# First attention: order of logits, values and other pieces on TensorE, and the banks they use

## The chip, the core and the metric

One core of a Trainium2 chip runs the whole program. Its engines are TensorE (PE: matrix products), VectorE (DVE), ScalarE (ACT), GpSimd (POOL) and SyncE (SP, which here only issues transfers). Each engine works through its own list of instructions in order and waits on semaphores for the others. TensorE writes its products into PSUM, which has eight banks of 128 partitions x 512 float32; the other operands lie in SBUF. The metric is the time of one execution in microseconds on the device. An execution is timed several times, and the median counts; one execution is also profiled.

## What is computed

Two transformer layers on x of 4 batches x 1024 rows x 256 columns, each with an attention and a mixture of experts, both behind a layer norm that is scaled and shifted per batch (adaLN). The change touches the first attention, in which 16 heads of 16 columns share one latent key and value of 64 columns:

```python
Q = (hidden_states @ Wq.T).reshape(b, t, h, d)
latent_k = hidden_states @ Wk_down.T
latent_v = hidden_states @ Wv_down.T
q_lat = jnp.einsum('bthd,hdl->bthl', Q, q_to_latent)
logits = jnp.einsum('bthl,bsl->bhts', q_lat, latent_k) / math.sqrt(l)
logits = jnp.where(causal[None, None], logits, jnp.float32(-1e+30))
attn = jax.nn.softmax(logits, axis=-1)
ctx_lat = jnp.einsum('bhts,bsl->bhtl', attn, latent_v)
heads = jnp.einsum('bhtl,hld->bthd', ctx_lat, v_up)
out = heads.reshape(b, t, h * d) @ Wout.T
```

The expert layer behind it takes the two best of 16 experts for each row: a router's logits, a softmax, a sort of the rows by expert, then two products per row with a layer norm and a gelu between. Its routing and sorting for the batches that are ready are done while the attention still works on the later batches.

## The kernel before

**Units.** The kernel multiplies the key and value weights into 256-column ones once, so that a head has 16 key columns and 16 value columns of its own. It goes through 4 batches x 2 halves of the heads (`g`) x 2 sets (`o`: the even or the odd ones of the eight heads of a half) x 9 units: 144 units, in the list `units` (L436). A unit (`UNITS`, L232) is a block of 512 columns of queries against one block of 128 keys, or two smaller blocks that together have 512 columns, for four heads at once. `scores` (L380) makes the logits of a unit with 4 or 8 products that each use 32 rows of the array, into two tiles `ps_s` of two banks each (L383); ACT takes the exponential of each of the two tiles into a tile `pT` (L396, 7 buffers), and POOL sets the upper triangle to 0 in the diagonal units (L399).

**Sums.** `sums` (L441) is a generator over the value products in order. One chunk, 512 queries of four heads, is accumulated in one bank `ps_av` (L448): 4 or 8 pieces of a unit, listed in `SUMS` (L244), each of four products that use 32 columns of the array (L453). Before each piece it yields the number of the unit whose exponentials the piece needs. When the chunk is complete, `finish` (L407) transposes it on DVE (L411), takes the reciprocal of the sums of the exponentials (L413) and scales (L414); every second time it transposes back (L416). At the end of a batch the generator appends the projection (`project`, L420) and, through `after_batch`, the routing of the batch (`Experts0.rows`, L1101) and after every second batch the sort (`Experts0.sort`, L1117) to the list `around`.

**Other work.** `around` is a list of generators, and a step (`Around.step`, L44) runs the first of them to its next `yield`. Between two yields lies a piece. Large pieces are the products for the values (`ps_v`, L349), for queries and keys (`ps_qk`, L364) and of the projection (`ps_out`, L427), each filling one bank. Small ones are the transpositions of normalised rows (`ps_lnT`, L153 and L1057), the router's products (`ps_route`, L794, and `ps_logits`, L802) and the sort's (`ps_rank`, `ps_expert`, `ps_gain`). Others only give work to DVE (statistics, normalising). `prepare` (L341) for the next half of the heads is put at the head of the list. Besides, `riders` scatter the sorted rows to memory, one transfer from POOL's queue for each step (L1158, L964); each is tied to the logits before it by `paced` (L980).

**Banks.** `ps_s` has three tiles of two banks, `ps_o` one bank for the sums, `ps_m` one for the other work. A `Spread` object (L275) hands out the tile for a piece: during the first and the last part (`early`) three of four come from `ps_s`, in the loop all from `ps_m`.

**Order.** An ordering pass, the planner, puts the instructions of each engine in an order of its own, by priority (their place in the text) and its own estimate of when each is ready. Inside `manual_schedule` the named engines keep the order of the text; before the change this is POOL alone. The loop (L472) does per turn: the value pieces of all units up to n - 2, the logits of unit n, one piece of other work (two in every fourth turn of the middle batches), one rider. After the loop come the last values, the projection of the last batch, and the experts (`Experts0.run`, L1178), whose weights are loaded by SP into memory that the attention leaves.

Of the kernel before, what the change touches and what calls it, by code (L numbers as in the profile page):

```python
# [8 lines left out]
F32 = mybir.dt.float32  # L9
# [4 lines left out]
PSUM = bass.MemoryType.PSUM  # L14

P = 128
B, N, C = 4, 1024, 256
NT = N // P
CC = C // P
# [14 lines left out]
class Around:  # L34
# [9 lines left out]
    def step(self, pieces=1, rides=1):  # L44
        pieces -= self.over
        while pieces > 0 and self.tasks:
            done = next(self.tasks[0], None)
            if done is None:
                self.tasks.pop(0)
            else:  # L50
                pieces -= done
        self.over = max(-pieces, 0)
        for _ in range(rides):
            if self.riders and next(self.riders[0], self) is self:
                self.riders.pop(0)

    def finish_tasks(self):
        while self.tasks:
# [192 lines left out]
def attention0(ctx, k, a, after_batch=lambda b: None):  # L251
# [18 lines left out]
    k.work = work = ctx.enter_context(k.tc.tile_pool(name="a0_work", bufs=2, reuse_waits="tile"))  # L270
    ps_s = ctx.enter_context(k.tc.tile_pool(name="a0_ps_s", bufs=3, space=PSUM, reuse_waits="tile"))
    ps_o = ctx.enter_context(k.tc.tile_pool(name="a0_ps_o", bufs=1, space=PSUM, reuse_waits="tile"))
    ps_m = ctx.enter_context(k.tc.tile_pool(name="a0_ps_m", bufs=1, space=PSUM, reuse_waits="tile"))

    class Spread:  # L275


        early, turn = True, 0

        def tile(self, shape, dtype, tag=None, name=None):  # L280
            self.turn += 1
            if self.early and self.turn % 4:
                full = ps_s.tile([P, 2, 512], dtype, tag="s", name=name)[:, 0, :]
            else:
                full = ps_m.tile([P, 512], dtype, tag="m", name=name)
            size = 1
            for n in shape[1:]:
                size *= n
            full = full[: shape[0], :size]
            if len(shape) == 2:  # L290
                return full
            names = "abc"[: len(shape) - 1]
            return full.rearrange(
                f"p ({' '.join(names)}) -> p {' '.join(names)}", **dict(zip(names, shape[1:]))
            )
# [1 line left out]
    misc = Spread()  # L297


    raw = work.tile([L, 4, C], F32, tag="pT", name="raw", bufs=7)  # L300
    wkd, wvd, q2l, vup = (raw[:, i, :] for i in range(4))
    for dst, name in ((wkd, "wkd"), (q2l, "q2l"), (wvd, "wvd"), (vup, "vup"), (wq, "wq"), (wo, "wo")):
        nc.scalar.dma_start(dst, a[name])
    k.load_c()

    def load_mod(layer):
        rest = work.tile([P, 2, 512], F32, tag="pT", name="mod_rows", bufs=7)
        w = []
        for i in range(3):
            w.append(work.tile([P, CC, 512], F32, tag="pT", name="wmod", bufs=7))  # L310
            nc.sync.dma_start(w[i], a[f"wmod{layer}"][:, :, i * 512 : (i + 1) * 512])
        return w, rest[:, 0], rest[:, 1, :C], rest[:, 1, C:]

# [66 lines left out]
    def scores(b, g, o, u):  # L380
# [11 lines left out]
                ).ins  # L392
        pTs = []
        for ps in pair:
            pT = work.tile([P, 2, 512], F32, tag="pT", name="pT", bufs=7)
            nc.scalar.activation(pT, ps, AF.Exp, scale=1.0 / L**0.5)  # L396
            for _, _, c0, _, diagonal in UNITS[u]:
                if diagonal:
                    nc.gpsimd.affine_select(  # L399
                        out=pT[:, :, c0 : c0 + P], in_=pT[:, :, c0 : c0 + P],  # L400
                        compare_op=ALU.is_ge, fill=0.0, base=0,
                        pattern=[[0, 2], [1, P]], channel_multiplier=-1,
                    )
            pTs.append(pT)
        return pTs

    def finish(b, g, o, qc, po, onT):  # L407


        turned = work.tile([P, 16, 32], F32, tag="turned", name="turned")  # L410
        nc.vector.transpose(turned.rearrange("p n d -> p (n d)"), po)  # L411
        rec = recs[:, 8 * b + 4 * g + 2 * o + qc].rearrange("p i j -> p (i j)")
        nc.vector.reciprocal(rec, turned[:, :, D])  # L413
        nc.vector.tensor_tensor(mixed[qc][:, :, o], turned[:, :, :D], bcast(rec, 2, D), ALU.mult)  # L414
# [26 lines left out]
    def sums():  # L441

        for b in range(B):
            on = ons[b % 2]
            for g in range(2):
                for o in range(2):
                    for qc, pieces in enumerate(SUMS):
                        po = ps_o.tile([P, 512], F32, tag="o", name="ps_av")  # L448
                        for n, (u, i) in enumerate(pieces):
                            yield place[b, g, o, u]  # L450
                            kb, _, c0, w, _ = UNITS[u][i]
# [14 lines left out]
    k.around.finish_tasks()  # L466
    setup_mod(k, 1, misc, mod)
    misc.early = False
    with k.tc.manual_schedule(engines={mybir.EngineType.Pool}):
        summing = sums()  # L470
        wanted = next(summing)
        for n, (b, g, o, u) in enumerate(units):  # L472
            if n == 8:
                k.clear_rows()
            if (o, u) == (0, 0):
# [2 lines left out]
                coming = (b, 1) if g == 0 else (b + 1, 0)  # L478
                if coming[0] < B:
                    around.insert(0, prepare(*coming))  # L480
            while wanted is not None and wanted <= n - 2:
                wanted = next(summing, None)
            exps[b, g, o, u] = scores(b, g, o, u)
            k.around.step(2 if b in (1, 2) and n % 4 == 3 else 1)
        misc.early = True
        for _ in summing:
            pass
        while projects[-1] in around:
# [587 lines left out]
class Experts0:  # L1076
# [24 lines left out]
    def rows(self, b, scalar):  # L1101

        k, rt = self.k, self.rt
        hf, i = divmod(b, HB)
        if i == 0:
            self.scale, self.shift = (
                spread_rows(k, rt, 0, part, 1, name, HB * hf, HB)
                for part, name in ((SCALE, "scale_f0"), (SHIFT, "shift_f0"))
            )
            self.logits = rt.tile([P, HT, E0], F32, tag="logits", name="logits")  # L1110
        statistics = yield from row_statistics(k, self.work, b)
        yield from routed_rows(
            k, self.work, b, statistics, self.scale[:, i], self.shift[:, i],
            self.wr, self.br, E0, self.logits[:, i * NT : (i + 1) * NT], scalar,
        )

# [1070 lines left out]
```

## Time and profile before

| What | us |
|---|---|
| runs | 1089.41, 1083.16, 1086.05 |
| median of the runs | 1086.05 |
| profiled execution | 1087.63 |
| its span | 1085.8 |
| first logits of the loop start | 45.1 |
| last values of the attention start | 507.0 |
| TensorE busy from 40 to 510 us | 454.0 of 470 |
| ACT, DVE and POOL busy from 40 to 510 us | 295.7, 180.2, 145.1 |
| granted TensorE clock from 40 to 510 us | 0.99 of full speed |

The span is the time from the first to the last recorded instruction; the execution's time has 1.8 us more around it. Times in the traces are microseconds from the span's start. A matrix product in float32 leaves two records, so a piece of four products has eight (x8). The ends of products are modelled by the profiler, since they run in a pipeline; what can be trusted is the distance from one start to the next. A releaser behind an arrow (<-) is the instruction whose end ended a wait.

### The profile page before, as it was taken

The numbers are of one execution on the slowest core, as the hardware profiler recorded it, in microseconds if no ns is written. First come the engines' busy times: TensorE is split into PE (matmuls) and PEld (weight loads), VectorE is DVE, ScalarE is ACT, GpSimd is POOL, SyncE is SP. The second block draws the span as 40 slices with busy tenths as digits, with TensorE's granted clock in tenths as the row PEclk, the third lists the DMA queues.
The fourth block names the chain that finished last, engine by engine and source line by source line (L and its number), as shares of the span: only waits on it lengthen the run. The fifth ranks groups of instructions, "written<-read, shape, count | busy, mean of one in ns | idle before, by whom it ended". The sixth has DMA issues, their size and how long they took to land.

```text
span 1085.8 us, 18090 instructions
## 1 busy us (share of the span) xinstructions
PE 945.7 (87%) x6072; PEld 559.8 (52%) x6072; DVE 620.4 (57%) x1987; ACT 602.5 (55%) x959; POOL 336.0 (31%) x528
## 2 busy tenths in 40 slices
PE   4899999999999999889679989986997989858760
PEld 2434434443443434335568878874464656547550
DVE  5822235422465155413676767993899968564572
ACT  0368655765477555775555657766654745523430
POOL 2013211311232234663004615612550100553632
PEclk9999999999999999999899999998999899989875
DMA  6995000100010001552825556624223201458764
GB/s 206 358 346 179 1 1 6 40 1 1 1 64 1 1 30 54 201 215 78 317 88 170 197 177 189 196 75 144 67 65 148 88 2 39 141 170 264 240 205 130
DMA packets 97142, 132.89 MB, mean 122 GB/s; under 512 B 8536, under 2 KB 84216, under 8 KB 96528
## 3 DMA queue, kind: packets, MB, share of 16 engines
q1 hardware_dynamic: 84656, 97.27, 26.9%
q0 software_dynamic: 11776, 33.57, 9.9%
q8 instruction: 52, 0.85, 0.3%
q10 hardware_dynamic: 608, 0.79, 0.3%
q14 instruction: 50, 0.41, 0.1%
HBM read 67.85 MB, written 63.75 MB: 121 GB/s over the span
## 4 chain that ended last, share of the span: by engine, by line
PE 63%; DVE 19%; issue 5%; DMA 5%; ACT 4%; POOL 1%; SPq 1%; DVEq 0%; ACTq 0%; POOLq 0%
PE ps_s L388 13%; PE ps_av L453 12%; PE ps_qk L364 6%; PE ps_y L1312 5%; PE ps_h L1247 4%; PE ps_v L349 3%; PE ps_out L427 3%; PE ps_pr L1609 3%; PE ps_y L1938 3%; PE ps_q L1537 2%; PE ps_k L1511 2%; DVE y L1601 2%; DMA ys<-results,index 2%; PE ps_lnT L1057 1%; DVE st L1258 1%
## 5 line engine op out<-in xcount | busy, mean ns | idle before, releaser
L396 ACT ACTIVATE pT<-ps_s 128x1024 f32<-128x1024 f32 x288 | 279.3, 1022 | 169.7 <-PE ps_s L388 167.2
L399 POOL TENSOR_SCALAR_AFFINE_SELECT pT<-pT 128x256 f32<-128x256 f32 x256 | 104.2, 431 | 328.4 <-ACT pT L396 323.7
L388 PE MATMUL ps_s<-qT,kT 32*128 32x512 f32 (+3 forms) x1536 | 178.8, 523 | 0.1
L453 PE MATMUL ps_av<-pT,v 128*32 128x512 f32 (+3 forms) x1536 | 165.2, 497 | 9.4 <-DVE turned L411 5.6
L964 POOL DMA_INDIRECT sorted<-hs,index x96 | 96.2, 1002 | 144.9 <-PE ps_y L1312 73.0
L974 POOL DMA_INDIRECT ys<-results,index x96 | 102.7, 1070 | 119.0 <-DMA results<-y 43.6
L388 PEld LDWEIGHTS ps_s<-qT,kT 32*128 32x128 f32 x1536 | 74.5, 185 | 95.5 <-issue 72.8
L453 PEld LDWEIGHTS ps_av<-pT,v 128*32 128x32 f32 x1536 | 40.6, 108 | 104.0 <-issue 58.7
L1247 PE MATMUL ps_h<-w,xT 128*128 x352 | 82.1, 386 | 6.5 <-DVE mv L1259 3.8
L1312 PE MATMUL ps_y<-w,act 128*128 x352 | 83.7, 392 | 4.2 <-DVE rs_seed L84 2.8
L411 DVE STREAM_TRANSPOSE turned<-ps_av 128x512 f32<-128x512 f32 x32 | 22.8, 712 | 98.9 <-PE ps_av L453 98.6
L1312 PEld LDWEIGHTS ps_y<-w,act 128*128 128x128 f32 x352 | 67.7, 197 | 14.0 <-ACT act L1295 4.8
L1247 PEld LDWEIGHTS ps_h<-w,xT 128*128 128x128 f32 x352 | 66.2, 193 | 15.9 <-issue 4.2
L1295 ACT ACTIVATE act<-ps_hT,gain 128x128 f32<-128x128 f32 x176 | 63.6, 463 | 16.9 <-PE ps_hT L1286 16.8
L1270 ACT ACTIVATE hid<-hid,nmr,rstd 128x256 f32<-128x256 f32 x88 | 47.5, 603 | 39.4 <-DVE nmr L1263 39.2
L1511 PE MATMUL ps_k<-wqkv,hT 128*128 128x512 f32 x128 | 61.9, 603 | 3.6 <-DMA wqkv<-in_wqkv_dram 2.8
L1938 PE MATMUL ps_y<-we,xT 128*128 x200 | 53.0, 412 | 10.6 <-ACT xT L1930 8.4
L371 DVE COPY qT<-ps_qk 128x512 f32<-128x512 f32 x16 | 11.0, 688 | 81.8 <-PE ps_qk L364 81.8
L103 DVE BATCH_NORM_STATS2 ln_st<-x 128x6 f32<-128x256 f32 x128 | 49.2, 407 | 0.5
L1255 DVE TENSOR_TENSOR hid<-ps_h,b 128x256 f32<-128x256 f32 x88 | 33.9, 415 | 26.6 <-PE ps_h L1247 21.5
L1938 PEld LDWEIGHTS ps_y<-we,xT 128*128 128x128 f32 x200 | 38.2, 204 | 20.1 <-ACT xT L1930 11.6
L374 DVE TENSOR_SCALAR kT<-ps_qk,par 128x512 f32<-128x512 f32 x32 | 22.5, 745 | 37.0 <-PE ps_qk L364 37.0
(223 smaller groups left out, 1499.4 us busy)
## 6 DMA issues: line engine op xcount, KB each, us to landing
xs<-sorted SPq DMA_DIRECT2D x69, 256.0 KB, 3.8
results<-y SPq DMA_DIRECT2D x69, 256.0 KB, 3.0
sorted<-zero SPq DMA_DIRECT2D x2, 6016.0 KB, 20.1
rows_in<-h SPq DMA_DIRECT2D x16, 512.0 KB, 2.9
hs<-rows_in POOLq DMA_DIRECT2D x32, 256.0 KB, 3.5
w<-in_w_dram SPq DMA_DIRECT2D x8, 1024.0 KB, 11.3
x<-in_x_dram SPq DMA_DIRECT2D x4, 1024.0 KB, 6.5
b<-in_b_dram SPq DMA_DIRECT2D x2, 2048.0 KB
```

What stands on the lines that cost most here:

```text
L364: nc.tensor.matmul(ps, lhsT=w[:, cc, g * P : (g + 1) * P], rhs=hT[:, cc, hf * 512 : (hf + 1) * 512], start=cc == 0, stop=cc == CC - 1,)
L388: k.anchor = nc.tensor.matmul(pair[hh // 2][:, hh % 2, c0 : c0 + w], lhsT=kTs[o][rows, kb * P : (kb + 1) * P], rhs=qT[rows, q1 - w : q1], ...
L396: nc.scalar.activation(pT, ps, AF.Exp, scale=1.0 / L**0.5)
L399: nc.gpsimd.affine_select(out=pT[:, :, c0 : c0 + P], in_=pT[:, :, c0 : c0 + P], compare_op=ALU.is_ge, fill=0.0, base=0, pattern=[[0, 2], [ ...
L453: nc.tensor.matmul(po[32 * hh : 32 * hh + 32, 512 - w :], lhsT=vs[b % 2][:, kb, 8 * g + 2 * hh + o, :], rhs=exps[b, g, o, u][hh // 2][:, h ...
L964: i = self.k.nc.gpsimd.indirect_dma_start(out=buffer.ap, out_offset=bass.IndirectOffsetOnAxis(ap=index, axis=0), in_=rows, in_offset=None, ...
L974: self.paced(self.k.nc.gpsimd.indirect_dma_start(out=rows, out_offset=None, in_=buffer.ap, in_offset=bass.IndirectOffsetOnAxis(ap=index, a ...
L1247: mm = nc.tensor.matmul(ph[:, j], lhsT=xTs[i // 2][:, j, cc], rhs=w1[:, cc, bass.ds(at[i + j], C)], start=cc == 0, stop=cc == CC - 1,)
L1295: o = nc.scalar.activation(act[:, j, cc], pt[:, j, cc], AF.Gelu, bias=gain[:, 1, cc, t : t + 1], scale=gain[:, 0, cc, t : t + 1],)
L1312: mm = nc.tensor.matmul(po[:, j], lhsT=acts[i // 2][:, j, cc], rhs=w2[:, cc, bass.ds(at[i + j], C)], start=cc == 0, stop=cc == CC - 1,)
L1511: k.anchor = nc.tensor.matmul(ps, lhsT=hT[:, cc, t * P : (t + 1) * P], rhs=wqkv[:, cc, C:], start=cc == 0, stop=cc == CC - 1,).ins
L1938: k.anchor = nc.tensor.matmul(po[:, j], lhsT=xT[:, j, cc], rhs=self.we[:, cc, bass.ds(at[j], C)], start=cc == 0, stop=cc == CC - 1,).ins
```

## The change

1. Sums and other work share two banks, `bank0` and `bank1`. Every chunk of the sums reverses the list: the sums take `banks[0]`, the other work `banks[1]`. In the loop the first piece of a turn uses `banks[1]`, the second a tile of `ps_s`.
2. The loop makes the logits of unit n first. Then, unless the last turn asks for a rest, and as long as the next value piece needs a unit later than n - 3, it runs other work until two pieces with a tile have been done, or one with a router's or sort's product that others wait for (`last`), or pieces without a tile worth more than 1. With a single task left it does one large piece only. Only in a turn without a tile do the values follow: of all units up to n - 1, or of unit n - 2 alone where that is the next. After a turn with small pieces the next one rests, which lets the values come.
3. TensorE too keeps the order of the text.
4. `pT` gets 8 buffers. The room for it comes from `turned` (one buffer instead of two) and from the rows of scale and shift for the expert layer's norm, which are loaded for each batch by itself instead of for two batches together.
5. The transposition of a finished chunk on DVE is given high priority.

```diff
+    def piece(self):
+        while self.tasks:
+            done = next(self.tasks[0], None)
+            if done is not None:
+                return done
+            self.tasks.pop(0)
+        return 0
...
-    ps_m = ctx.enter_context(k.tc.tile_pool(name="a0_ps_m", bufs=1, space=PSUM, reuse_waits="tile"))
+    banks = [ps_o.tile([P, 512], F32, tag=f"bank{i}", name=f"bank{i}") for i in range(2)]
     class Spread:
-        early, turn = True, 0
+        early, turn, large, last = True, 0, 0, False
         def tile(self, shape, dtype, tag=None, name=None):
             self.turn += 1
-            if self.early and self.turn % 4:
+            self.large += name in ("ps_v", "ps_qk", "ps_out")
+            self.last = name in ("ps_route", "ps_rank", "ps_expert")
+            if self.turn % 4 if self.early else self.turn % 2 == 0:
                 full = ps_s.tile([P, 2, 512], dtype, tag="s", name=name)[:, 0, :]
             else:
-                full = ps_m.tile([P, 512], dtype, tag="m", name=name)
+                full = banks[1]
...
-            pT = work.tile([P, 2, 512], F32, tag="pT", name="pT", bufs=7)
+            pT = work.tile([P, 2, 512], F32, tag="pT", name="pT", bufs=8)
...
-        turned = work.tile([P, 16, 32], F32, tag="turned", name="turned")
-        nc.vector.transpose(turned.rearrange("p n d -> p (n d)"), po)
+        turned = work.tile([P, 16, 32], F32, tag="turned", name="turned", bufs=1)
+        with k.tc.high_priority():
+            nc.vector.transpose(turned.rearrange("p n d -> p (n d)"), po)
...
-                        po = ps_o.tile([P, 512], F32, tag="o", name="ps_av")
+                        banks.reverse()
+                        po = banks[0]
...
-    with k.tc.manual_schedule(engines={mybir.EngineType.Pool}):
+    with k.tc.manual_schedule(engines={mybir.EngineType.Pool, mybir.EngineType.PE}):
         summing = sums()
-        wanted = next(summing)
+        wanted, rest = next(summing), False
         for n, (b, g, o, u) in enumerate(units):
...
-            while wanted is not None and wanted <= n - 2:
-                wanted = next(summing, None)
             exps[b, g, o, u] = scores(b, g, o, u)
-            k.around.step(2 if b in (1, 2) and n % 4 == 3 else 1)
+            misc.turn = misc.large = quiet = 0
+            misc.last = False
+            while not rest and wanted > n - 3 and misc.turn < 2 and not misc.last:
+                if misc.large and len(around) < 2:
+                    break
+                done = misc.turn
+                quiet += k.around.piece()
+                if misc.turn == done and (done or quiet > 1 or not around):
+                    break
+            k.around.step(0)
+            if not misc.turn:
+                end = n if wanted != n - 2 else n - 1
+                while wanted is not None and wanted < end:
+                    wanted = next(summing, None)
+            rest = misc.turn > misc.large and wanted < n
         misc.early = True
+        k.around.step(1, 0)
...
+        scale, shift = (
+            spread_rows(k, rt, 0, part, 1, name, b, 1)[:, 0]
+            for part, name in ((SCALE, "scale_f0"), (SHIFT, "shift_f0"))
+        )
         if i == 0:
-            self.scale, self.shift = (
-                spread_rows(k, rt, 0, part, 1, name, HB * hf, HB)
-                for part, name in ((SCALE, "scale_f0"), (SHIFT, "shift_f0"))
-            )
             self.logits = rt.tile([P, HT, E0], F32, tag="logits", name="logits")
         statistics = yield from row_statistics(k, self.work, b)
         yield from routed_rows(
-            k, self.work, b, statistics, self.scale[:, i], self.shift[:, i],
+            k, self.work, b, statistics, scale, shift,
```

## The prediction

> **What bounds the kernel now.** I read the page first (busy time, then the slices with the granted clock), then the chain of waits, then busy time by stretch, and last TensorE's timeline through the first attention, from start to start. The page says that TensorE is the engine to follow and the groups say where:
>
> ```profile
> PE 945.7 (87%) x6072; PEld 559.8 (52%) x6072; DVE 620.4 (57%) x1987; ACT 602.5 (55%) x959; POOL 336.0 (31%) x528
> ...
> L396 ACT ACTIVATE pT<-ps_s 128x1024 f32<-128x1024 f32 x288 | 279.3, 1022 | 169.7 <-PE ps_s L388 167.2
> ...
> L388 PE MATMUL ps_s<-qT,kT 32*128 32x512 f32 (+3 forms) x1536 | 178.8, 523 | 0.1
> L453 PE MATMUL ps_av<-pT,v 128*32 128x512 f32 (+3 forms) x1536 | 165.2, 497 | 9.4 <-DVE turned L411 5.6
> ```
>
> ACT's 279 us of exponentials waited 167 us for logits, TensorE almost never idled (0.1 and 9.4 us), so in this stage (45 to 507 us of the span, the only one that the diff reorders) TensorE's order sets the end. How far it could shrink is in the timeline of TensorE; the columns are start, duration, what:
>
> ```profile
> 92.78 1.14 PE L388 MATMUL ps_s<-qT,kT 32*128 32x512 f32 x8
> 93.85 1.06 PE L453 MATMUL ps_av<-pT,v 128*32 128x512 f32 x8
> 94.84 1.38 PE L388 MATMUL ps_s<-qT,kT 32*128 32x384 f32 x16
> 96.15 1.38 PE L453 MATMUL ps_av<-pT,v 128*32 128x512 f32 x8
> 97.46 1.14 PE L388 MATMUL ps_s<-qT,kT 32*128 32x512 f32 x8
> ...
> 119.23 1.15 PE L388 MATMUL ps_s<-qT,kT 32*128 32x384 f32 x16
> 120.31 1.99 PE L349 MATMUL ps_v<-wv,hT 128*128 128x256 f32 x8
> 122.23 1.06 PE L453 MATMUL ps_av<-pT,v 128*32 128x512 f32 x8
> ```
>
> The reader is to see the turn: logits 1.07, a large piece 1.92, values 0.99; and that without a piece two turns take 2.06 and 2.62, the second with 0.24 before half of the logits and 0.31 inside the values. Two kinds of neighbours price an opening, the cost of going from one kind of work to another:
>
> ```profile
> 29.66 5.34 PE L349 MATMUL ps_v<-wv,hT 128*128 128x256 f32 x24
> 34.84 3.60 PE L364 MATMUL ps_qk<-hT,wq 128*128 128x512 f32 x8
> 38.28 3.60 PE L364 MATMUL ps_qk<-hT,wk 128*128 128x512 f32 x8
> ...
> 86.97 1.50 PE L453 MATMUL ps_av<-pT,v 128*32 128x512 f32 x16
> 88.39 1.14 PE L388 MATMUL ps_s<-qT,kT 32*128 32x512 f32 x8
> ```
>
> Three large pieces in a row take 5.18, two 3.44: 1.72 each, so 0.20 of the 1.92 is opening. Values of 768 columns take 1.42 against 0.99 for 512: 0.43 per 256 columns, 0.86 per unit, opening 0.14. A small piece (four transposes) takes 0.59 after logits and, by the eight of ps_hT and ps_xT elsewhere (some 0.88 start to start), 0.44 as a second one.
>
> **The work, before and after.** Both loops can be followed on paper, since the order of pieces depends on counts alone. In 144 turns the old loop has 44 turns with one large piece, 4 with two, 35 with small ones only, 61 with none, and values in 142. The new one has 18 turns with two large, 16 with one, 15 with two small, 9 with one small, and 86 without pieces; only these 86 carry values (51 of about one unit, 7 of two, 28 of three). The same 52 large and 39 small pieces are done. Openings saved: values 142 - 86 = 56 x 0.14 = 7.8; second large pieces 18 - 4 = 14 x 0.20 = 2.8; second small ones about 1.5. Sum **-12.1 us of work**.
>
> **The waits before.** From the first logits of the loop (45.09) to the last (502.45) are 457.4 us. Adding 1.07 per turn, the values and the pieces at the prices above gives 414.4, so 43.0 are waits: 24.9 in turns without pieces, 12.2 in those with large ones (4.8 of it at the start, where logits at 48.26 are followed by the next only at 57.08), 5.9 beside small ones.
>
> **The waits after.** They are estimates from the rows.
> (a) The start: the second piece of K and Q waits for DVE's copy of the first, busy with the modulation rows; the change keeps order and bank: 4.8 (the same at both ends).
> (b) Turns without pieces. Of the old 60, four hold 10.6 us of special waits (below); the others wait (24.9 - 10.6) / 56 = 0.25. In the new order a value group stands behind the next logits, one unit further from its exponential, so waits for the select after the exponential go (the 0.31 above) and the logits' wait for the bank (0.24 each second turn, 0.12 a turn) stays. Between 0.12 and 0.25 I take 0.18: 61 such turns, 11.0 (7.3 to 15.3).
> (c) Turns with small pieces have no values beside them any more, and here the change adds a wait. The exponentials' rows
>
> ```profile
> 94.01 1.94 ACT L396 ACTIVATE pT<-ps_s 128x1024 f32<-128x1024 f32 x2 [0.38 <-PE ps_s L388]
> 96.14 1.94 ACT L396 ACTIVATE pT<-ps_s 128x1024 f32<-128x1024 f32 x2 [0.19 <-PE ps_s L388]
> ```
>
> start 1.23 after their logits, 0.97 apart, 1.02 long. There are three pairs of banks for logits. A second piece now takes the third pair, so the next logits need both exponentials: 1.23 + 0.97 + 1.02 + 0.06 = 3.28 after the last ones, where TensorE has 1.07 + 0.59 + 0.44 = 2.10 of work: 1.18 x 15 = 17.7. After one small piece only half of the next logits waits, for the first exponential, 2.31 against about 1.5: 0.8 x 9 = 7.2. In three turns a transposition and the routing product that reads its copy stand together; the planner used to put logits between them, the written order cannot, and ACT's copy comes behind both exponentials: 1 x 3. Sum 27.9 (20 if later turns catch some of it up).
> (d) Turns with large pieces: 0.8; two pieces last 3.64, longer than both exponentials.
> (e) The four special ones: 1.5 and 3.6 wait for the transposition of the sums (DVE had been given eight normalising instructions first); two banks and high priority take these away: 0. The other two, 2.9 and 2.6, are selects held on POOL behind a fetch of rows that waits for a scatter. The scatters go on, one a turn, from turn 112 instead of 107, and the extra unit of distance covers about half: 2.5 (0 to 5.5).
> (f) Pieces whose input DVE or ACT delivers late, since TensorE cannot pass them now: 2 (0 to 15, see the second rival).
> Sum 4.8 + 11.0 + 27.9 + 0.8 + 2.5 + 2 = 49.0, against 43.0: **+6.0 us**.
>
> **The rest at nothing.** The eighth exponentials' buffer only lets ACT run further ahead; ACT waits on POOL's buffers 1.1 us in all, which is all it can win. Scale and shift rows are now two loads of 128 KB a batch on SP instead of two of 256 KB per two batches; each may start once the batch before has normalised its rows, some 33 turns ahead, so they lie under the attention. Batch 3's come after the loop, beside w2 (4 x 1 MB, median 11.3 us to land); without that cover they are late by up to 8. The last scatter issues with the last logits: 1 + 4.7 + 3.8 us to its rows being back, against 11.3 us from those logits to the first use of rows at 513.78. I take 0 for both.
>
> **Sum.** -12.1 + 6.0 = -6.1. The profiled execution took 1087.63 (span 1085.8, 1.8 around it) and becomes 1081.5. It is 1.6 above the median of the runs, 1086.05, so for the median **1080**.
>
> **A price for long waits.** The clock speaks against an order with waits:
>
> ```profile
> 434.00:438.00 4.00, 0.81 (x20) 0.53 (x16) 3.86 (x8) 2.02 (x3) 3.83 (x7) 1.00 0.32 98
> 438.00:442.00 4.00, 4.00 (x32) 1.60 (x31) 0.69 (x2) 0.62 (x1) 1.45 (x3) 0.57 0.55 197
> ...
> 480.00:484.00 4.00, 3.49 (x32) 1.27 (x32) 0.00 (x0) 1.04 (x2) 3.65 (x9) 1.00 0.18 66
> ```
>
> After TensorE's 3.2 us wait at 434.7 the granted clock (third column from the right) is 0.57 for the next stretch; after the 2.2 us wait before 480.5 it stays at 1.00. The waits that I add are 1.2 and shorter, so I add nothing. The Trainium skill (TensorE: The Clock Gate, What's actually happening) says that an idle window of about 3.4 us halves the clock, until a window of like length has been busy; by it each wait of (f) that long would cost a further 1.7 us, an estimate from that page alone.
>
> **Rivals.**
> *Waits vanish too.* One unit more of distance and a second bank free TensorE of nearly all: (b) at 0.12, (c) at 20, (e) and (f) 0, 33 instead of 49: 1080 - 16 = **1064** at its end, 1070 in its middle. For it: the quiet pairs of 2.07 and 2.30 (at 147 to 151). Against: (c) is arithmetic on ACT's rows.
> *The written order waits for late results* (the other side). In at least six places of the old timeline the planner put logits ahead of a piece that stood before them in the text. Now TensorE stands still instead, and logits, hence exponentials, stand behind it. Its timeline has seven waits for DVE in this stage, 3.2, 3.1, 1.5, 1.0, 0.6, 0.5 and 0.5, mean 1.5. At the 15 turns of two small pieces, or equally often at copies of K and Q, two 0.75 us instructions each on a DVE planned by guess, 10 such waits cost 15: **1095**; from 8 on it is slower than before by over 0.5%.
> *The end gives it back.* Five turns later, the scatters and batch 3's scale rows come after TensorE wants them: some 6 of the 8, **1086**. Against: the 11.3 us of cover.
>
> **How the numbers follow.** Chances: forecast 0.45, vanish 0.20, late results 0.28, the end 0.07. 0.5%, 5.4 us, is about what this measurement can tell from no change (its runs lie within 0.3% of their median). The forecast's own range, 1075 to 1086, lies with 0.24 beyond 5.4 us faster and 0.21 within; vanish is all faster; late results all slower but 0.01; the end 0.02 faster, 0.04 within, 0.01 slower. So 0.46, 0.26, 0.28. The range takes in most of both sides: 1068 to 1096.
>
> **What would show it.** Right: values in groups of 1.00, 1.86 and 2.72; turns with two large pieces of 4.7; 86 value groups; logits after two small pieces starting about 3.3 after the ones before or split in halves; no wait for the transposed sums. Wrong: two large pieces 3.84 instead of 3.64 (no opening saved); waits over 1.5 us at pieces on DVE or ACT; a granted clock under 0.95 inside the stage; rows for the first experts later than 11.5 us after the last logits.

## The result and the profile after

The changed kernel takes 1090.10 us (median of 20 runs, 1087.19 to 1096.66) against 1087.08 (20 runs, 1082.98 to 1091.34) of the kernel before on the same chip: a ratio of 1.0034, 95% interval 1.0018 to 1.0051. So it is 3 us slower, and the forecast was 6 us faster. This is less than the 0.5% that the prediction named as its bound, but the interval leaves out no change. The profiled execution took 1095.42 (span 1093.6), at the upper end of the runs; another profile of the same kernel (below) took 1090.59.

The page of the changed kernel, with TensorE's line and the groups that answer to those shown of before:

```profile
PE 946.1 (87%) x6072; PEld 570.8 (52%) x6072; DVE 621.5 (57%) x1987; ACT 601.1 (55%) x959; POOL 335.5 (31%) x528
...
L409 ACT ACTIVATE pT<-ps_s 128x1024 f32<-128x1024 f32 x288 | 278.4, 1022 | 167.1 <-PE ps_s L401 163.6
...
L401 PE MATMUL ps_s<-qT,kT 32*128 32x512 f32 (+3 forms) x1536 | 188.6, 532 | 2.5 <-ACT pT L409 1.7
L468 PE MATMUL bank<-pT,v 128*32 128x512 f32 (+3 forms) x1536 | 150.3, 503 | 3.3 <-POOL pT L412 3.3
```

The values went from 165.2 to 150.3 us of busy time, and their idle time from 9.4 (5.6 of it for `turned`) to 3.3: grouping and two banks do what they were to do. Yet ACT waits for logits nearly as long as before (163.6 us for 167.2). Part of what took the gain back stands in the logits' own line, 188.6 us for 178.8: where the second half of a unit's logits waits, the view shows no idle time but a longer stretch of products (one of 2.04 us in place of 1.14 is shown below), and a lower clock lengthens it too. The rest isn't in these groups. The stretch from the first to the last logits of the loop, and from there to the experts' first rows (`ps_xT`), is next; columns: window, length, busy time of PE, PEld, DVE, ACT and POOL, granted clock, DMA share, GB/s. First the kernel before:

```profile
45.09:502.45 457.36, 442.26 (x3548) 181.62 (x3549) 172.52 (x422) 292.62 (x316) 142.80 (x293) 0.99 0.23 79
502.45:513.78 11.33, 11.33 (x76) 8.06 (x73) 6.33 (x19) 3.05 (x4) 2.35 (x6) 1.00 0.10 26
```

and the changed kernel:

```profile
45.60:506.69 461.09, 437.39 (x3540) 188.87 (x3540) 173.61 (x422) 291.64 (x317) 136.38 (x289) 0.97 0.22 74
506.69:519.97 13.28, 12.25 (x84) 7.84 (x81) 6.69 (x19) 2.81 (x3) 6.86 (x11) 1.00 0.45 149
```

TensorE is busy for 4.9 us less, those longer stretches included, but it stands idle for 461.09 - 437.39 = 23.7 us where it stood 15.1, at a clock of 0.97 for 0.99. So the loop is 3.7 us longer. The list of TensorE's waits in the changed kernel (us in total, times, longest) says for what:

```profile
PE ps_route L827 <- ACT hT L1101: 4.9, 3, 1.6
PE bank L1090 <- DVE turned L425: 4.8, 1, 4.8
PE bank L1090 <- DVE h L1070: 3.6, 4, 1.0
...
PE bank L468 <- POOL pT L412: 3.3, 3, 2.3
...
PE bank L928 <- DVE some L923: 1.4, 1, 1.4
```

With 0.3 for the experts' product (L982) that is 4.9 + 4.8 + 3.6 + 1.4 + 0.3 = 15.0 us in ten waits for a result that DVE or ACT had not finished, all at pieces of routing and sort. In the kernel before the pieces of routing and sort waited 1.9 us, 1.0 of it at `ps_gain`, 0.6 at `ps_expert` and 0.3 at `ps_lnT`. TensorE's timeline in the changed kernel shows one such place:

```profile
187.29 1.15 PE L401 MATMUL ps_s<-qT,kT 32*128 32x384 f32 x16
188.37 0.44 PE L1090 MATMUL bank<-ident,h 128*128 128x128 f32 x2
189.85 0.33 PE L1090 MATMUL bank<-ident,h 128*128 128x128 f32 x1 [1.04 <-DVE h L1070]
190.93 0.48 PE L1090 MATMUL bank<-ident,h 128*128 128x128 f32 x1 [0.76 <-DVE h L1070]
191.20 1.06 PE L1090 MATMUL ps_lnT<-ident,h 128*128 128x128 f32 x4
192.19 2.08 PE L401 MATMUL ps_s<-qT,kT 32*128 32x256 f32 x16
```

Two row blocks of `h` are transposed, then TensorE waits for each further one, and the next logits, which need nothing of it, start at 192.19. The largest wait is on DVE's side of the timeline:

```profile
439.21 0.62 DVE L1067 SCALAR_TENSOR_TENSOR h<-x,ln_mv,scale_f 128x256 f32<-128x256 f32 x1
439.86 1.15 DVE L1070 SCALAR_TENSOR_TENSOR h<-h,ln_rstd,shift_f 128x256 f32<-128x256 f32 x1
440.93 0.70 DVE L425 STREAM_TRANSPOSE turned<-bank 128x512 f32<-128x512 f32 x1
```

From 431.95 to 440.9 DVE does eight such pairs; only then the transposition of the sums (L425), which frees the bank that the routing's transposition writes. TensorE waits 4.84 us for it, until 441.69. The high priority didn't prevent this; no run leaves it out, so what it does by itself isn't shown.

### The profile page after: what moved, and what is told of

It reads as the page before. It is cut to its first block, busy times and chain, and to the rows that moved or that the text cites. A ratio compares the mean times of both kernels' runs of the same rounds, so it can differ in the third digit from the quotient of the medians.

```text
span 1093.6 us, 18127 instructions
## 1 busy us (share of the span) xinstructions
PE 946.1 (87%) x6072; PEld 570.8 (52%) x6072; DVE 621.5 (57%) x1987; ACT 601.1 (55%) x959; POOL 335.5 (31%) x528
## 4 chain that ended last, share of the span: by engine, by line
PE 64%; DVE 18%; DMA 5%; ACT 5%; issue 5%; POOL 1%; SPq 0%; DVEq 0%; ACTq 0%; POOLq 0%
PE ps_s L401 14%; PE bank L468 11%; PE ps_y L1345 5%; PE ps_h L1280 5%; PE bank L377 4%; PE ps_pr L1642 3%; PE ps_k L1544 2%; PE ps_y L1971 2%; DMA ys<-results,index 2%; PE ps_q L1570 2%; PE ps_qk L377 2%; PE bank L362 2%; PE ps_out L441 1%; DVE y L1634 1%; PE ps_v L362 1%
## 5 line engine op out<-in xcount | busy, mean ns | idle before, releaser
L409 ACT ACTIVATE pT<-ps_s 128x1024 f32<-128x1024 f32 x288 | 278.4, 1022 | 167.1 <-PE ps_s L401 163.6
L401 PE MATMUL ps_s<-qT,kT 32*128 32x512 f32 (+3 forms) x1536 | 188.6, 532 | 2.5 <-ACT pT L409 1.7
L468 PE MATMUL bank<-pT,v 128*32 128x512 f32 (+3 forms) x1536 | 150.3, 503 | 3.3 <-POOL pT L412 3.3
L401 PEld LDWEIGHTS ps_s<-qT,kT 32*128 32x128 f32 x1536 | 77.8, 188 | 96.5 <-issue 44.5
L425 DVE STREAM_TRANSPOSE turned<-bank 128x512 f32<-128x512 f32 x32 | 22.9, 716 | 133.1 <-PE bank L468 133.1
L468 PEld LDWEIGHTS bank<-pT,v 128*32 128x32 f32 x1536 | 42.1, 111 | 102.8 <-issue 74.9
L1971 PE MATMUL ps_y<-we,xT 128*128 x200 | 54.4, 420 | 12.8 <-ACT xT L1963 10.2
L1354 DVE TENSOR_TENSOR y<-ps_y,b 128x256 f32<-128x256 f32 x88 | 35.2, 418 | 15.6 <-PE ps_y L1345 13.9
L384 DVE COPY qT<-bank 128x512 f32<-128x512 f32 x11 | 7.6, 690 | 61.6 <-PE bank L377 44.7
```

Source lines behind the costliest of these rows:

```text
L401: k.anchor = nc.tensor.matmul(pair[hh // 2][:, hh % 2, c0 : c0 + w], lhsT=kTs[o][rows, kb * P : (kb + 1) * P], rhs=qT[rows, q1 - w : q1], ...
L468: nc.tensor.matmul(po[32 * hh : 32 * hh + 32, 512 - w :], lhsT=vs[b % 2][:, kb, 8 * g + 2 * hh + o, :], rhs=exps[b, g, o, u][hh // 2][:, h ...
L1971: k.anchor = nc.tensor.matmul(po[:, j], lhsT=xT[:, j, cc], rhs=self.we[:, cc, bass.ds(at[j], C)], start=cc == 0, stop=cc == CC - 1,).ins
```

## The experiments

Theory A: the written order makes TensorE stand before results that come late, and the clock falls after it. Theory B: the turns of small pieces, which now carry no values, cost it. Theory C: the end costs it (scatters, POOL's queue). Theory D: a fixed order as such costs, at many places. All ratios are to runs of the kernel before on the same chip; "stage" is the first to the last logits, "end" the last logits to the first `ps_xT`, both of the profiled execution.

| Run | median us | ratio, 95% interval | stage | end |
|---|---|---|---|---|
| before | 1087.08 | | 457.4 | 11.3 |
| changed | 1090.10 | 1.0034 (1.0018 to 1.0051) | 461.1 | 13.3 |
| e1_late_rows | 1075.15 | 0.9894 (0.9871 to 0.9917) | 440.6 | 16.5 |
| e2_planned_order | 1083.25 | 0.9969 (0.9951 to 0.9987) | 452.9 | 11.9 |
| e3_before_fixed_order | 1092.79 | 1.0039 (1.0026 to 1.0053) | 461.9 | 11.8 |
| e4_small_with_values | 1079.76 | 0.9935 (0.9915 to 0.9956) | 445.5 | 18.6 |
| e5_late_and_values | 1065.30 | 0.9796 (0.9772 to 0.9821) | 430.3 | 19.0 |
| e6_two_riders | 1089.16 | 1.0013 (0.9998 to 1.0027) | 461.9 | 11.7 |
| e7_seven_buffers | 1089.96 | 1.0021 (1.0001 to 1.0041) | 456.9 | 13.3 |
| e9_late_values_two_riders | 1079.05 | 0.9905 (0.9882 to 0.9928) | 450.4 | 11.7 |
| e10_one_turn_products_stay | 1072.14 | 0.9866 (0.9839 to 0.9893) | 442.5 | 11.9 |
| e11_one_turn_later | 1064.95 | 0.9788 (0.9759 to 0.9817) | 429.7 | 16.7 |
| e12_late_products | 1081.02 | 0.9944 (0.9925 to 0.9964) | 449.4 | 12.1 |
| e13_late_transposition | 1085.39 | 0.9979 (0.9963 to 0.9996) | 449.5 | 16.7 |
| e14_best_fetch_first | 1063.34 | 0.9782 (0.9756 to 0.9809) | 427.2 | 17.9 |
| e15_fetch_first | 1088.89 | 1.0024 (1.0009 to 1.0040) | 460.2 | 11.9 |
| e16_changed_again | 1090.59 (one) | | 460.0 | 11.9 |

One and the same order of TensorE gave stages of 461.1, 460.0 and, with seven buffers, 456.9, and ends of 13.3, 11.9 and 13.3. So some 4 us between two stages, or 1.4 between two ends, say nothing by themselves.

**The late pieces, moved.** A `yield 2` without a piece ends a turn's other work. The parameter `late` is given by `Experts0.rows` alone, 0 for the last batch.

```diff
     h = yield from normalised(0)
+    for _ in range(late):
+        yield 2
     for q in range(2):
...
+        if late and q:
+            yield 2
         yield from route_logits(k, hT, wr, br, ne, work, logits[:, 4 * q : 4 * q + 4])
...
+            late=0 if scalar else 2,
```

> The changed kernel, in which the routing's first transposition of a batch comes two turns later and its second products one turn later, so that VectorE has its normalised rows ready; no work is added. Theory A (TensorE's written order stands waiting for late results: in the changed kernel's profile 2.6 us at 188, 2.7 us at 310 and 5.6 us at 441, and the clock falls after each): 8 to 14 us less than the changed kernel, 1076 to 1082. Theory B (the turns of small pieces without values cost it) and theory C (the end of the stage costs it): within 3 us of the changed kernel, 1087 to 1093.

It took 1075.15, 15 us less than the changed kernel and 11 less than before, a little past A's range; B and C alone are out. All ten waits are gone (a new one of 1.6 us stands at the sort's product `ps_expert`), and the place shown above runs through:

```profile
191.31 1.14 PE L401 MATMUL ps_s<-qT,kT 32*128 32x512 f32 x8
192.38 0.65 PE L1092 MATMUL bank<-ident,h 128*128 128x128 f32 x4
192.87 0.60 PE L1092 MATMUL ps_lnT<-ident,h 128*128 128x128 f32 x4
193.64 2.04 PE L401 MATMUL ps_s<-qT,kT 32*128 32x512 f32 x8 [0.17 <-ACT pT L409]
```

Its stage in the view by windows:

```profile
44.71:485.29 440.58, 432.26 (x3548) 188.84 (x3548) 171.20 (x422) 290.65 (x316) 135.40 (x286) 1.00 0.23 77
```

Idle time fell from 23.7 to 8.3 us, by 15.4. The same work also took 432.26 in place of 437.39 busy us, as the clock stayed at 1.00: 5.1 more. The end took 3.2 back.

**The two parts of it alone.** The lines of the diff above, one at a time (for the products `late=not scalar` without the first loop; for the transposition without `if late and q`).

> The changed kernel with only the routing's second products one turn later; the transposition stays where it was. Theory A by its rows: the three waits of 1.62 us go and the low clock behind them (1.6 us each in two places of one execution) with them, the waits at the transposition (2.6, 2.7, 5.6 us) stay: 4 to 8 us less than the changed kernel, 1082 to 1086.

> The changed kernel with only the routing's first transposition two turns later; the products stay right behind the second transposition. Theory A by its rows: 10.9 us of waits at the transposition go, the three of 1.62 stay: 8 to 12 us less than the changed kernel, 1078 to 1082. With the run before this one the two gains should add to the 15 us of both edits together.

The sizes missed on both sides (9 us less and 5 less than the changed kernel), their sum, 14, fits. The waits explain both. With the products moved, the later pieces shift too: the transposition that waited 4.84 us at 441.69 comes one turn later and that wait is gone, so this run had more than its own. With the transposition moved, its waits are gone and the stage is 11.5 us shorter, but one new wait appears among e13's waits, and the end is 3.4 us longer:

```profile
PE ps_route L827 <- ACT hT L1103: 4.8, 3, 1.6
PE bank L377 <- DVE chosen L1187: 3.9, 1, 3.9
```

`chosen` is the sort's work on DVE. What frees the bank for the queries and keys is the transposition of the sums, which by DVE's timeline stands behind that work, from 396.55 to 397.26, just ahead of the product at 397.31. In a written order a shift of one turn makes and unmakes such meetings.

**The order by itself.** Two runs change only who orders TensorE.

```diff
-    with k.tc.manual_schedule(engines={mybir.EngineType.Pool, mybir.EngineType.PE}):
+    with k.tc.manual_schedule(engines={mybir.EngineType.Pool}):
```

> The changed kernel with TensorE's order left to the planner again. Its order differs from the written one at a few places only: the set-up, and three places where the routing's products behind a transposition of the same turn come half with and half after the first logits of the next turn. Theory A expects only those three waits of 1.6 us and the low clock behind two of them (1.6 and 1.7 us more) to shrink, 3 to 8 us less than the changed kernel, 1082 to 1087, and the waits at the transposition (2.6, 2.7, 5.6 us) unchanged. Theory D (the fixed order as such costs it, at many places): back to the time before or below, with those waits gone too. Theories B and C: no difference from the changed kernel.

```diff
-    with k.tc.manual_schedule(engines={mybir.EngineType.Pool}):
+    with k.tc.manual_schedule(engines={mybir.EngineType.Pool, mybir.EngineType.PE}):
```

> The kernel before with TensorE's order also written by hand, nothing else. Its loop writes values and pieces in another order than the planner at some ten places; the routing's products come right behind the transposition. Theory A (a written order costs where a late result stands in it, and here three products would then wait 1 to 1.6 us and little else): 1 to 6 us slower than before. Theory D (a written order costs or gains at many places): 8 us or more to either side.

The first is 7 us under the changed kernel, in A's range, and the waits moved as A said: those for `hT` fell from 4.9 to 1.2 us, those at the transposition stayed to the tenth:

```profile
PE bank L1090 <- DVE turned L425: 4.8, 1, 4.8
...
PE bank L1090 <- DVE h L1070: 3.6, 4, 1.0
...
PE ps_route L827 <- ACT hT L1101: 1.2, 3, 0.5
```

But they make 3.7 of the 8.2 us by which the stage is shorter. Another 4.7 come at its start, which no theory named: the planner takes a piece for the queries ahead of the first logits, the wait for `qT` falls from 3.1 to 0.9 us, and the fourth logits start 9.28 us after the first, for 13.97 in the changed kernel. So the total's place in A's range is in part luck.

The second, the kernel before with a written order and nothing else, is 4 to 5 us slower than before, by new waits in its list of the loop's waits:

```profile
PE ps_route L794 <- ACT hT L1068: 4.0, 2, 2.0
...
PE ps_out L427 <- DVE kT L374: 3.0, 2, 1.5
...
PE ps_v L349 <- ACT hT L162: 2.2, 1, 2.2
```

These three make 9.2 us and the stage grew by 4.5, so the written order also saved something, which wasn't followed up. D's 8 us or more didn't come: as far as these waits show, the fixed order costs what stands late in it. The Trainium skill (PSUM — Partial Sum Buffer, Engine vs sequencer instructions) says that TensorE's products start and complete in the order of its program; these lines agree, since only the planner's order, not the chip, got past a late product.

**Values also in turns of small pieces.**

```diff
-            if not misc.turn:
+            if not misc.large:
```

> The changed kernel with a due group of values also in a turn that held small pieces only. Theory B (logits wait 1.18 us each in turns of two small pieces because nothing covers the exponentials): the first to the last logits 7 us shorter by following the loop with the step times, 1081 to 1085 in all. Theory A: no wait at the transposition goes, so it stands within 3 us of the changed kernel, unless B holds beside it.

1079.76, 10 us less than the changed kernel and a little below B's range: B holds beside A. The changed kernel's timeline at two small pieces (the second logits split, 2.04 long, since they need both exponentials):

```profile
101.01 0.60 PE L162 MATMUL ps_lnT<-ident,ln_xn 128*128 128x128 f32 x4
101.54 2.04 PE L401 MATMUL ps_s<-qT,kT 32*128 32x512 f32 x8
103.51 2.36 PE L468 MATMUL bank<-pT,v 128*32 128x512 f32 x32
```

and the same pieces with values behind them, in e5:

```profile
101.26 0.60 PE L162 MATMUL ps_lnT<-ident,ln_xn 128*128 128x128 f32 x4
101.79 1.07 PE L468 MATMUL bank<-pT,v 128*32 128x512 f32 x8
102.78 1.14 PE L401 MATMUL ps_s<-qT,kT 32*128 32x512 f32 x8
```

The values fill 0.99 us in which TensorE stood between the halves of the logits. The stage fell by 15.6 where 7 were expected: the wait of 4.84 for `turned` happens to be gone here too, while those for `h` grew from 3.6 to 7.2 us, and the end took 5.3 back.

> Both edits: the routing's pieces later and the values also in turns of small pieces. If A and B hold beside each other their gains add: 13 to 20 us less than the changed kernel, 1070 to 1077, under the kernel before. A alone: as the first of these runs, 1076 to 1082. B alone: 1081 to 1085.

1065.30: 24.8 us less, about the sum of 15.0 and 10.3 and more than the 13 to 20 expected. Both causes hold beside each other, but they aren't independent: in the stage the two edits alone gave 20.5 and 15.6 us and together 30.8, as e4 had lost the wait for `turned` too. What values in turns of small pieces bring where the ten late waits are gone is the difference from e1 to e5, 10.3 us of the stage and 9.9 in all; the logits' line falls from 191.1 to 177.8 us of busy time with it.

**The end.** Three runs change only POOL's transfers, on the changed kernel or on e5's.

```diff
-            k.around.step(0)
+            k.around.step(0, 1 + n % 2)
```

> The changed kernel with two scattered blocks in every second turn in place of one in each, so that the scatters are issued before the last logits; TensorE's order is the same. Theory C (the late scatters cost the end: the last logits to the first rows of the experts 13.3 us where the kernel before took 11.3, and a value group waits 2.3 us for POOL at 496): 3 to 5 us less than the changed kernel, 1085 to 1087. Theory A alone: the sum of the end is 2 us, so 0 to 2 us less. If POOL's selects come behind two scatters in a turn: up to 5 us slower.

> Late routing pieces, values also in turns of small pieces, and two scattered blocks in every second turn. If the end gave back part of the stage's gain only through the late scatters (in the run with the first two edits the last logits to the first rows took 19.0 us, with POOL waits of 1.3 and 3.3 us and the rows' load 0.7): 4 to 7 us less than that run's 1065.3, 1058 to 1061. If the selects come behind two scatters: 1065 or more.

On the changed kernel 1 to 2 us less, inside A's range; the intervals of the two overlap. On top of e5's two edits it cost 12 to 14 us, the other outcome that was named: waits of value groups for POOL's selects rose from 4.6 us to

```profile
PE bank L468 <- POOL pT L412: 12.8, 5, 4.9
```

and the stage from 430.3 to 450.4. POOL's timeline in the changed kernel shows what stands there; TensorE's values of 495.84 waited 2.28 us for this select:

```profile
490.69 1.01 POOL L997 DMA_INDIRECT sorted<-hs,index  x1 [0.18 <-issue]
494.61 0.75 POOL L1198 DMA_DIRECT2D hs<-rows_in  x1 [2.92 <-DMA sorted<-hs,index]
495.36 1.48 POOL L412 TENSOR_SCALAR_AFFINE_SELECT pT<-pT 128x256 f32<-128x256 f32 x4
```

The fetch of new rows waits until the scatter just issued has landed, and the selects queue behind it. So the fetch was put ahead of a scatter:

```diff
                 for s in range(2):
+                    if (i, s) == (1, 1) and t + 4 < HT:
+                        coming.append(fetch(t + 4))
                     self.sorting.scatter(hs[:, i], k.sorted0[hf], index[:, s, t + i : t + i + 1])
-                    if (i, s) == (1, 0) and t + 4 < HT:
-                        coming.append(fetch(t + 4))
                     yield
```

> The changed kernel in which the fetch of the next rows is issued on POOL just ahead of a scatter, a turn after the scatter before it, in place of right behind one; every other engine's order is the same. In the changed kernel's profile such fetches stand 2.0 to 2.9 us on POOL until the scatter has landed, and selects and value groups stand behind them (2.3 us at 496, 0.5 and 0.5 at 509 and 511). Theory C: those 3.3 us and the clock behind them go: 3 to 6 us less than the changed kernel, 1084 to 1087. Theory A: at most those 3.3: 1087 to 1090.

1 us less, A's range and within the intervals, but the edit doesn't touch what it was aimed at. POOL's timeline in this run:

```profile
487.33 1.01 POOL L997 DMA_INDIRECT sorted<-hs,index  x1 [0.30 <-issue]
492.03 0.75 POOL L1198 DMA_DIRECT2D hs<-rows_in  x1 [3.70 <-DMA sorted<-hs,index]
492.79 1.48 POOL L412 TENSOR_SCALAR_AFFINE_SELECT pT<-pT 128x256 f32<-128x256 f32 x4
```

This fetch waits 3.7 us, and a value group behind it 3.1 where 2.3 had been, but it isn't one of those that the edit moves. Of the first half's rows there are eight fetches, two at the start and six between its scatters. In the changed kernel all eight stand for nothing (0.00), the last one at 488.94, right behind a scatter. The three that wait there (494.61, 505.49 and 515.43) come after these eight, so by count they are the first three of the second half. Each stands behind the last scatter from one of the three buffers of `hs`, which it is to fill. So the run doesn't measure what the fetches cost. For C in the changed kernel there remain its own rows, 2.28 + 0.49 + 0.54 = 3.3 us of value groups waiting for POOL in the first profile.

**One turn is enough.** The edit of e1 with `late=0 if scalar else 1`, with values also in turns of small pieces (e11), the same without the products' delay (e10), and e11 with the fetch ahead of a scatter (e14).

> Late pieces as in the first run but the transposition one turn later in place of two, the products one turn later, values also in turns of small pieces. The scatters begin one turn earlier than with two turns (114 for 115 by following the loop). If one turn is enough for VectorE's four normalising pairs: 1063 to 1066, as the best run or a little less. If not, the waits at the transposition come back in part: 1068 to 1072.

> The transposition one turn later, the products where they were, values also in turns of small pieces. The scatters begin at turn 112. If the end after the last logits is set by the scatters, it is 3 to 6 us shorter than the 19.0 us of the run with both edits, and the three waits of 1.62 us for the products cost 5 to 8: 1063 to 1070. If the start of the scatters sets nothing: 1070 to 1074.

> The best run so far (one turn later, products late, values also in turns of small pieces) with the fetch ahead of a scatter. If the end's give-back (the last logits to the experts' first rows 16.7 us, a value group waiting 3.4 us for a select behind a fetch, then 3.98 us for 2.7 us of values) comes from the fetches on POOL: the end 4 to 5 us shorter, 1059 to 1062. If the end is set by the number of scatters left: 1064 to 1066.

One turn does (1064.95). With the products left behind the transposition, `hT` costs 4.6 us again in three waits and the clock is 0.98 instead of 1.00, and the stage is 12.8 us longer, where 5 to 8 were expected; its scatters begin two turns earlier and the end is 11.9 instead of 16.7, so 7 us remain. The total is that of e10's second reading, the short end that of its first. Moving the fetch gave 1.6 us, within the intervals. A value group behind the last logits still waits 3.8 us for POOL, behind a fetch of the second half that the edit leaves where it was (479.22, itself 3.0 us late). So neither reading of e14 is settled and what the end could give stays open. Its 1063.34 is the fastest time, 2.2% under the kernel before.

**The eighth buffer.** All `bufs=8` of the tag `pT` back to 7.

> The changed kernel with seven exponentials' buffers in place of eight; every engine's order is the same. The prediction took the eighth at nothing: within 2 us of the changed kernel. If the eighth is what carries a group of three behind its exponentials, every such turn (some 28) waits for a buffer: 5 to 20 us slower.

1089.96: nothing, as predicted. The loading of scale and shift by batch wasn't tried by itself.

**The changed kernel once more.**

> The changed kernel once more, for its profile alone. If the low clock behind short waits (at 192, 212, 315 in the first profile; not in the run with seven buffers, whose orders and waits are the same) is a matter of the execution and not of the order, it is at other places or missing here, and the time lies elsewhere between 1087 and 1097. If it belongs to the waits, it is at the same three places.

The waits at routing and sort are the same to 0.01 us, the clock isn't (POOL's waits differ, 3.3 and 2.5 us). Windows of the first profile:

```profile
188.00:192.00 4.00, 2.21 (x20) 1.47 (x12) 3.83 (x10) 2.50 (x3) 2.38 (x5) 0.84 0.06 16
192.00:196.00 4.00, 4.00 (x34) 1.93 (x32) 2.60 (x6) 2.24 (x4) 0.53 (x2) 0.73 0.42 144
...
210.00:214.00 4.00, 3.68 (x36) 1.56 (x40) 0.29 (x1) 1.89 (x3) 0.80 (x3) 0.65 0.00 0
```

and of the second, whose times are 0.5 us and 2 us earlier at these places:

```profile
188.00:192.00 4.00, 2.21 (x24) 1.44 (x23) 3.86 (x9) 3.02 (x4) 2.05 (x4) 1.00 0.18 60
192.00:196.00 4.00, 4.00 (x46) 1.68 (x40) 2.42 (x6) 3.51 (x4) 1.76 (x4) 1.00 0.37 127
...
210.00:214.00 4.00, 4.00 (x24) 0.87 (x16) 0.00 (x0) 1.82 (x2) 1.53 (x4) 0.58 0.00 0
```

After the wait of 190 the clock fell in one and stayed in the other; after the 1.62 us of 208 to 210 it fell in both, and in the run with seven buffers, with the same orders and the same waits, it fell at neither place (1.00 from 188 to 218). Behind the two waits of 1.04 and 0.75 us at 310 to 313 it fell in the first profile alone.

## Why the prediction was wrong

"Work" is each run's own order at the prediction's prices. The waits of each class are the distances from logits to logits less that work, so they hold low clock, and any error of the prices, too:

| us | predicted | changed | changed again | e1 | e14 |
|---|---|---|---|---|---|
| work | 402.3 | 401.3 | 401.3 | 401.7 | 404.9 |
| large pieces and start (a), (d) | 5.6 | 5.8 | 5.8 | 5.8 | 7.0 |
| no pieces, not behind small ones (b), (e) | 13.5 | 10.8 | 12.5 | 7.0 | 6.6 |
| small pieces and the turn behind them (c), (f) | 29.9 | 43.2 | 40.4 | 26.1 | 8.7 |
| first to last logits | 451.3 | 461.1 | 460.0 | 440.6 | 427.2 |

**The work** was right: by the order as it ran, 13.1 us saved for 12.1 predicted, and the prices hold where nothing waits. Groups of values of 512, 768 and 1536 columns take 1.00, 1.43 and 2.72, a turn with two large pieces 4.7.

**The step that failed is (f)**, "Pieces whose input DVE or ACT delivers late, since TensorE cannot pass them now: 2 (0 to 15, see the second rival)". The rows give 15.0 us in ten waits (some 3 of it counted in (c) for `hT`), and moving just these pieces took 15 us off the whole. The second rival had the mechanism, the number and the mean (10 waits x 1.5 = 15); it looked for them at copies of keys and queries as well, which wait 0.4 us behind the start, and they were all at routing and sort. That ten and 1.5 both came out is in part luck: one wait of 4.84 is a third of the sum, the other nine have a mean of 1.1. Its total of 1095 was too high, mostly because (b) and (e) came out smaller and some 3 of the 15 already stood in (c). It should have been the forecast: the prediction itself counted that the planner had moved at least six such pieces, and DVE's rows give the price. The eight pairs from 431.95 to 440.9 make 4.5 us for four, and by the loop two of the four pairs that a transposition needs are handed to DVE in the turn before it and two in the same turn, where a turn lasts 2 to 3 us.

**The clock at nothing** failed too. "The waits that I add are 1.2 and shorter" held for those of (c) only. In the stage the clock is 0.97 in the first profile and 0.98 in the second, for 1.00 in e1; in the first one that is worth about the 5.1 us of busy time shown there, and it differs from execution to execution.

**(c) was right**: 27.9 predicted, 26.1 in e1, where the ten late waits are gone. But it was a cost of one line, not of the design: in e14 8.7 of it are left, for 3.2 us more work than in e1. **(a), (d)** were right, though e2 shows that the start's 4.8 can go. **(b), (e)** were on the high side in sum, and POOL's part came as described, 2.28 us at 495.84 for 2.5. But (e) also had that two banks and high priority take the waits for the sums' transposition away, and that failed: no group of sums waits for `turned`, but other work does, 4.84 + 0.52 us where the kernel before had 5.6. The wait moved with the bank. The 4.84 is counted in (f) above.

**The rest at nothing.** Right for the buffer. The end took 2.0 us more in the first profile and 0.6 in the second for 0 predicted, so the third rival's 6 us didn't come in the changed kernel. They came in the faster ones: e1's end is 5.2 us longer than that of before, e5's 7.7. That a shorter loop leaves the same scatters less cover would explain it, but no run shows it: the scatters also begin later there, in turn 117 in e1 for 112 in the changed kernel.

**Waits vanish too** (1064) is about where the kernel stands once both causes are removed: 1063 to 1065.

## What to carry to other kernels

When an order is written by hand, list for each piece which engine makes its input, how long that takes and how many turns before it was issued; here four pairs of 1.1 us on DVE, handed over in the turn before and in the same one, came late, and one turn more was enough (e11). Else the engine stands, and everything behind it too. A planner's order that differs from the text is a list of the places where this matters. Price a stage's edits by one run for each suspected wait: the named waits told the sign here, while totals of single edits misled by what they shifted elsewhere, and check in the trace that the edit moves the instruction that waits.

## What the runs showed of the hardware

The granted clock fell behind short waits: to 0.58 to 0.65 over 4 us after one of 1.62 us, and to 0.73 after two of 1.04 and 0.76 us, with no longer wait beside them. And it did so by execution: the same program, with equal waits, lost it at 190 and at 210 in one profile, at 210 alone in another. The Trainium skill (TensorE: Matmul & The Clock Gate, What's actually happening) speaks of an idle window of about 3.4 us that runs freely, not tied to the program's start. In the traces each of these falls is a half clock for 3.41 us, and the falls of one profile lie whole multiples of 3.41 us apart (190.72, 211.20 and 313.60 in the first: 6 and 30 times). So these windows run freely here too, and where a wait lies in them changes with the execution. That an idle stretch as long as the window is needed doesn't agree with these waits, and the measurement decides: in the 3.41 us ahead of the first two falls TensorE stood idle for 1.6 us. A wait of 1.6 us can cost as much again (the group of three values behind it took 3.87 us from start to start for 2.72, the logits before it 1.56 for 1.08). How much idle time suffices stays open: with seven buffers a wait of 1.62 us, wholly inside one such window by that profile's own falls (207.44 to 210.85), left the clock at 1.00. On POOL, fetches into a buffer that a scatter still read stood 2.0 to 3.7 us in the changed kernel and e15, until that scatter had landed; fetches right behind a scatter from another buffer stood for nothing.
